# The order of the key tiles in a causal polynomial attention, and the engine of half of its masks

## The chip, the core and the metric

The kernel runs on one core of a Trainium2 chip. Time is device time in microseconds (us) for one launch, on the slowest core, which here is the only one. Lower is better. Before the change the median of three runs is 2473.38 us (2469.45 to 2477.04).

## What is computed

One block of a network on `x` of shape (4, 1024, 256), four sub-layers one after the other, each with a layer norm ahead of it and a residual sum behind it: a causal attention, a mixture of experts (16 experts, the best 6 for each token, and a shared one), a short convolution over the batch axis, and the same mixture once more. The attention has 16 heads of 16 numbers, rotary angles, a layer norm of each head's q and k, and a fourth power in place of the softmax:

```python
a = jnp.einsum('bhnd,bhmd->bhnm', q, k) ** degree      # degree = 4
a = jnp.tril(a)
denom = jnp.sum(a, axis=-1, keepdims=True)
return jnp.einsum('bhnm,bhmd->bhnd', a / denom, v)
```

So no maximum is subtracted and nothing runs along a row: the sums over keys may be taken in any order. The change touches the attention alone.

## The kernel before

**Tiling of the attention.** There are 8 pairs `u`: 4 batch rows by 2 groups of 8 heads. The 1024 queries are cut into an early half (`hf = 0`) and a late half (`hf = 1`) of 512. A *pass* is one pair and one half; the 8 early passes come first, then the 8 late ones. Within a pass the even and the odd heads (`a = 0, 1`) are done one after the other, four heads at a time; I call each of these a *list*. So there are 16 early lists and 16 late ones. A list runs over the key tiles `j` of 128 keys: four in the early half, eight in the late half. One key tile of one list is a *step*. Keys after a query do not count, so for the diagonal tiles (`j >= 4*hf`) only the queries from `n0 = (j - 4*hf)*128` on are computed: such a step is 512, 384, 256 or 128 queries wide, and its first 128 columns are masked. In the late half `j = 0..3` are 512 wide and unmasked. Before the change a list goes through `j` in rising order, so it ends on its narrow steps.

**One step.** `scores` (L686 and on) makes four matmuls, one for each head, on four strips of 32 rows of TensorE (L694), into two PSUM tiles `ps` of two heads each; there are only two such buffers, so the next step's scores must wait until ScalarE (ACT) has squared both of this step's tiles (L705). Then, for the diagonal steps, the first tile is masked on VectorE (DVE) by a product with the 0/1 tile `seen` (L712), and the second on GpSimd (POOL) by an `affine_select` (L714). The second squaring makes the fourth power: in the late half the first tile on DVE (L725), the second on ACT (L863); in the early half tile and parity of `j` decide among DVE, ACT and POOL (L727). `weigh` (L734 and on) multiplies by the values, four matmuls into one accumulator `acc` (L742), and after the last step of the list ACT copies `acc` out to `o_sb` (L751), which frees it for the next list. TensorE then turns `o_sb` into `po` (L764).

**The order of the work.** PE, DVE, ACT and the DMA queue of SP run in the order in which the program is written; so does POOL here in effect. Each turn of the main loop (L856 to L884) writes: the scores and first squares of step s+2 (`LOOK = 2`) with their masks and DVE squares; then some pieces of other work; then the ACT second square of step s+1 (L863); then `weigh` of step s; then more pieces of other work. An engine that waits for one operand holds up all that is written behind it on that engine.

**The other work** is cut into "bites" that are dealt out by the turn, not by time: the projections of q, k, v for a later pass (L571, two of four in each of two turns), their rotation and head norm on DVE (L593 to L623, with a root on ACT at L662), the transposes, the output projection (L794), and in the late half also the routing of the first half of the tokens for the mixture of experts (L273 to L391) and the scatter of their rows to the experts' queues in memory. These scatters are 96 indirect DMAs that POOL issues (L421), each about 1 us of POOL time. In the late half a chain for the next pass begins at the fourth step of a pass (`begin_chain`, L841).

The mixture stages after the attention (from about 765 us) are not touched.

Of the kernel before, what the change touches and what calls it, by code (L numbers as in the profile page):

```python
# [103 lines left out]
def block_kernel(  # L104
# [342 lines left out]
    with ExitStack() as actx:  # L447
# [238 lines left out]
        def scores(u, hf, a, j, last):  # L686

            n0 = max(0, (j - 4 * hf) * P)
            nq = 512 - n0
            kt = kT[u, j // 4]  # L690
            tiles = [PS["s"].tile([P, 2, 512], FP, tag="s", name="ps") for _ in range(2)]

            for h in (2, 0, 1, 3):
                nc.tensor.matmul(  # L694
                    tiles[h // 2][:, h % 2, 0:nq],
                    lhsT=kt[32 * h : 32 * h + 32, (j % 4) * P : (j % 4 + 1) * P],
                    rhs=qT[u, hf][a][32 * h : 32 * h + 32, n0:512],
                    start=True,
                    stop=True,
                )  # L700
            s2s, later = [], []
            masked = j >= 4 * hf
            for pr in range(2):
                s2 = sqp.tile([P, 2, 512], FP, name="s2")
                nc.scalar.activation(s2[:, :, 0:nq], tiles[pr][:, :, 0:nq], AF.Square)  # L705
                s2s.append(s2)
            for pr in range(2):
                s2 = s2s[pr]
                if masked:

                    if pr == 0:
                        nc.vector.tensor_mul(s2[:, :, 0:P], s2[:, :, 0:P], seen)  # L712
                    else:
                        nc.gpsimd.affine_select(  # L714
                            out=s2[:, :, 0:P],
                            in_=s2[:, :, 0:P],
                            compare_op=ALU.is_ge,
                            fill=0.0,
                            base=0,
                            pattern=[[0, 2], [1, P]],  # L720
                            channel_multiplier=-1,
                        )
                part = s2[:, :, 0:nq]
                if pr == 0 and (hf == 1 or j % 2 == 0):
                    nc.vector.tensor_mul(part, part, part)  # L725
                elif pr == 1 and hf == 0 and j % 2 == 1:
                    nc.gpsimd.tensor_mul(part, part, part)  # L727
                else:
                    later.append(part)
            return s2s, later  # L730
# [77 lines left out]
        passes = [(hf, u) for hf in range(2) for u in range(n_pairs)]  # L808

        def begin_chain(n):  # L810

            hf, u = passes[n]
            l, gp = pairs[u]
            if gp == 0:
                bites.need(NORM, (l, hf))
            bites.add(gp, qkv_bites(u, hf), n)
            if gp == 1 and n + 1 < len(passes):
                hf, u = passes[n + 1]
                l = pairs[u][0]
                bites.add(NORM, norm_bites(l, hf), (l, hf))  # L820


        later, powers = [], {}
        steps = [
            (n, a, j, 4 * hf + 3)
            for n, (hf, u) in enumerate(passes)
            for a in range(2)
            for j in range(4 * hf + 4)
        ]

        def forward(i):

            n, a, j, last = steps[i]
            hf, u = passes[n]
            if a == 0 and j == 0:
                bites.need(pairs[u][1], n)
            if hf == 0 and a == 1 and j == 0:
                begin_chain(n + 2)
            if hf == 1 and u > 0 and a == 0 and j == 3 and n + 1 < len(passes):

                begin_chain(n + 1)  # L841
            return scores(u, hf, a, j, last)

        with tc.manual_schedule(engines=ORDERED):
            with tc.tile_pool(name="ps_s", bufs=2, space=PSUM) as s, tc.tile_pool(
# [10 lines left out]
                for s in range(-LOOK, len(steps)):  # L856
                    bites.begin()
                    new = []
                    if s + LOOK < len(steps):
                        powers[s + LOOK], new = forward(s + LOOK)  # L860
                    bites.step(1, (1, 1, 1, 1, 1))
                    for part in later:
                        nc.scalar.activation(part, part, AF.Square)  # L863
                    later[:] = new
                    if s < 0:
                        bites.step(1, (2, 2, 1, 2, 1))
                        continue
                    n, a, j, last = steps[s]
                    hf, u = passes[n]
                    o_sb = weigh(u, hf, a, j, last, powers.pop(s))  # L870
                    bites.step(1, (2, 2, 1, 2, 1 if 0 not in plans or s % 2 else 0))
                    if o_sb is not None:
                        l, gp = pairs[u]
                        done = gather_bites(u, hf, a, o_sb)
                        if gp == 1 and a == 1:
                            done = chain(done, project_bites(l, hf))
                        bites.add(OUT, done)
                    if hf == 1 and not routed and not bites.lanes[OUT]:

                        routed = True  # L880
                        for i in range(TG):
                            bites.add(ROUTE, prepare(0, i, ap1, ps_m))
                        bites.add(ROUTE, chain(plan(0, ps_m), scatter(0, ap2, 1)))
# [437 lines left out]
```

## Time and profile before

| what | value |
|---|---|
| median of three runs | 2473.38 us |
| the profiled execution: its own time / its span | 2393.24 us / 2391.5 us |
| attention, first to last score (early half / late half) | 33.7 to about 285 us / 285 to 759 us |
| busy share of the span: PE, ACT, DVE, POOL | 88%, 52%, 47%, 38% |
| masks on DVE (L712), late half | 64, mean 427 ns |
| masks on POOL (L714), late half | 64, mean 687 ns |
| scatters issued by POOL (L421) in the attention | 96, mean 1048 ns |

The profiled execution took 80 us less than the median of the timed runs. The sums below are made against the profiled execution and then moved to the median.

A group line of the profile reads: line, engine, operation, output<-inputs, shape, count | busy us, mean ns of one | idle time of the engine just before, and which instruction's end released it. A timeline line reads: start, length, engine, line, operation, operands, count, and in brackets the idle time ahead and its releaser. The table of stretches gives for each stretch its length, then the busy time of each engine with its number of instructions in brackets, the clock granted to TensorE (1.00 is full), the DMA share and GB/s. A matmul's length in the timeline includes time in which its group waits for the second of its two PSUM tiles.

### The profile page before, as it was taken

To read this page: it belongs to the slowest core of one execution; us is meant where nothing else is said; L and a number is where in the kernel's file an instruction comes from. 1 tells how busy PE (TensorE), PEld (TensorE's weight loads), DVE (VectorE), ACT (ScalarE), POOL (GpSimd) and SP (SyncE) were. 2 spreads that over 40 slices of the span, in tenths; PEclk is the share of its full clock that TensorE was granted. 3 is DMA by queue.
4 is the path that set the end of the run, shared out by engine and by line. 5 is a ranking of instruction groups with operands and counts; after the bars stand their busy time and mean duration, and the time that the engine had idled before them with its cause. 6 is when DMAs were issued, how large, how long until landed. Compare 5 with 4: busy or idle time off the path is not lost.

```text
span 2391.5 us, 33033 instructions
## 1 busy us (share of the span) xinstructions
PE 2114.5 (88%) x10480; PEld 1308.4 (55%) x10480; DVE 1118.5 (47%) x2532; ACT 1240.2 (52%) x2754; POOL 901.4 (38%) x990
## 2 busy tenths in 40 slices
PE   5899999778898998999899999789999959999974
PEld 2344443222233466777666667567676747777632
DVE  5888867656555225111166652126754212441154
ACT  3677878566676145555455544335553424555410
POOL 3333211344431000444355226645513654540176
PEclk8888988889888999999999999989999979999987
DMA  7900000111101412555455335344423535663243
GB/s 232 342 7 1 1 1 1 38 51 45 53 27 62 114 48 79 165 166 166 137 151 154 102 104 176 132 139 142 145 92 121 176 124 154 202 186 115 91 123 112
DMA packets 212231, 267.73 MB, mean 112 GB/s; under 512 B 25280, under 2 KB 187232, under 8 KB 212064
## 3 DMA queue, kind: packets, MB, share of 16 engines
q1 hardware_dynamic: 166944, 161.04, 21.6%
q0 software_dynamic: 36992, 100.78, 13.4%
q10 hardware_dynamic: 8128, 3.80, 0.7%
q8 instruction: 91, 1.49, 0.3%
q14 instruction: 76, 0.62, 0.1%
HBM read 123.72 MB, written 141.82 MB: 111 GB/s over the span
## 4 chain that ended last, share of the span: by engine, by line
PE 67%; DVE 12%; issue 7%; ACT 7%; POOL 5%; DMA 2%; ACTq 0%; POOLq 0%; DVEq 0%; SPq 0%
PE pgu L1030 20%; PE py L1053 14%; PE ps L694 6%; PE acc L742 4%; PE pxt L1014 4%; PE pht L1044 4%; POOL xq L421 3%; PE pg L955 3%; ACT s L705 3%; PE pj L571 3%; PE pu L955 3%; PE po L972 3%; POOL yg L1147 2%; ACT s L863 1%; DVE X L1131 1%
## 5 line engine op out<-in xcount | busy, mean ns | idle before, releaser
L421 POOL DMA_INDIRECT xq<-sxn,sloti x384 | 379.2, 987 | 644.7 <-ACT xgT L1016 306.2
L1030 PE MATMUL pgu<-wgu,xgT 128*128 x1776 | 609.7, 466 | 4.4 <-DVE hbuf L1039 2.2
L1147 POOL DMA_INDIRECT yg<-yq,sloti x384 | 375.8, 979 | 421.8 <-issue 201.4
L1039 DVE TENSOR_TENSOR hbuf<-hbuf,pgu 128x176 f32<-128x176 f32 x444 | 149.4, 337 | 721.7 <-ACT hbuf L1038 721.2
L1030 PEld LDWEIGHTS pgu<-wgu,xgT 128*128 128x128 f32 x1776 | 338.7, 193 | 136.5 <-issue 20.3
L1038 ACT ACTIVATE hbuf<-pgu 128x176 f32<-128x176 f32 x444 | 141.4, 318 | 411.7 <-PE pgu L1030 411.6
L705 ACT ACTIVATE s<-ps 128x1024 f32<-128x1024 f32 (+3 forms) x384 | 291.4, 815 | 114.6 <-PE ps L694 113.5
L1053 PE MATMUL py<-w2a,hT 128*128 x888 | 268.7, 385 | 0.9 <-ACT yo L1062 0.9
L1053 PE MATMUL py<-w2b,hT 128*128 x888 | 266.4, 382 | 0.0
L1062 ACT COPY yo<-py 128x256 f32<-128x256 f32 x444 | 166.1, 374 | 167.0 <-PE py L1053 166.7
L1131 DVE SCALAR_TENSOR_TENSOR X<-yg,top,X 128x256 f32<-128x256 f32 x384 | 186.0, 484 | 87.8 <-DMA yg<-yq,sloti 81.8
L1014 PE MATMUL pxt<-ident,xg 128*128 128x128 f32 x888 | 171.8, 276 | 60.6 <-DMA xg<-xq 60.6
L714 POOL TENSOR_SCALAR_AFFINE_SELECT s<-s 128x256 f32<-128x256 f32 x128 | 84.2, 659 | 349.7 <-ACT s L705 349.5
L725 DVE TENSOR_TENSOR s<-s 128x1024 f32<-128x1024 f32 (+3 forms) x160 | 168.2, 1051 | 86.8 <-ACT s L705 83.5
L1016 ACT COPY xgT<-pxt 128x256 f32<-128x256 f32 x444 | 167.9, 378 | 68.7 <-PE pxt L1014 68.3
L694 PE MATMUL ps<-q,kA 32*128 32x512 f32 (+3 forms) x1024 | 182.0, 647 | 20.0 <-ACT s L705 18.0
L1044 PEld LDWEIGHTS pht<-ident,hbuf 128*128 128x128 f32 x888 | 125.9, 142 | 124.4 <-issue 71.1
L1053 PEld LDWEIGHTS py<-w2b,hT 128*128 128x128 f32 x888 | 170.2, 192 | 23.5
L863 ACT ACTIVATE s<-s 128x1024 f32<-128x1024 f32 x192 | 164.4, 856 | 27.5 <-POOL s L714 27.2
L1044 PE MATMUL pht<-ident,hbuf 128*128 128x128 f32 x888 | 171.6, 275 | 4.9 <-ACT hT L1046 4.9
L1046 ACT COPY hT<-pht 128x256 f32<-128x256 f32 x444 | 165.4, 372 | 1.7 <-PE pxt L1014 0.7
L742 PE MATMUL acc<-s,vA 128*32 128x512 f32 (+3 forms) x1024 | 140.1, 603 | 13.2 <-ACT s L863 10.8
(158 smaller groups left out, 2421.9 us busy)
## 6 DMA issues: line engine op xcount, KB each, us to landing
xg<-xq SPq DMA_DIRECT2D x148, 384.0 KB, 3.7
yq<-yo SPq DMA_DIRECT2D x148, 384.0 KB, 2.8
xq<-zero SPq DMA_DIRECT2D x74, 384.0 KB, 4.6
xq<-sxn,sloti POOLq DMA_INDIRECT x384, 2.4
yg<-yq,sloti POOLq DMA_INDIRECT x384, 2.9
wgu<-in_w SPq DMA_DIRECT2D x4, 1408.0 KB, 17.8
X<-in_x SPq DMA_DIRECT2D x8, 512.0 KB, 5.5
out<-X SPq DMA_DIRECT2D x8, 512.0 KB, 3.5
```

The lines of the kernel that those rows point to most:

```text
L421: d = nc.gpsimd.indirect_dma_start(out=xq[g][:, :], out_offset=bass.IndirectOffsetOnAxis(ap=sloti[:, c + i, k : k + 1], axis=0), in_=xs[:, ...
L694: nc.tensor.matmul(tiles[h // 2][:, h % 2, 0:nq], lhsT=kt[32 * h : 32 * h + 32, (j % 4) * P : (j % 4 + 1) * P], rhs=qT[u, hf][a][32 * h : ...
L705: nc.scalar.activation(s2[:, :, 0:nq], tiles[pr][:, :, 0:nq], AF.Square)
L725: nc.vector.tensor_mul(part, part, part)
L742: nc.tensor.matmul(acc[32 * r : 32 * r + 32, n0:512], lhsT=va[:, j % 4, h * VW : h * VW + 32], rhs=s2s[r // 2][:, r % 2, 0 : 512 - n0], st ...
L863: nc.scalar.activation(part, part, AF.Square)
L1014: nc.tensor.transpose(pt[:, k, :], xg[c][:, k * P : (k + 1) * P], ident)
L1030: nc.tensor.matmul(pg, lhsT=xT[c][:, k, :], rhs=wgu_f[k][:, bass.ds(vals[0] * (2 * FI), 2 * FI)], start=(k == 0), stop=(k == 1),)
L1044: nc.tensor.transpose(pt[:, k, :], hbuf[c % 4][:, k * P : (k + 1) * P], ident)
L1053: nc.tensor.matmul(py, lhsT=hT[c][:, k, :], rhs=w2_f[k][:, bass.ds(off[c] * E, E)], start=(k == 0), stop=(k == 1),)
L1131: nc.vector.scalar_tensor_tensor(X[:, t, l, :], yg[:, k, :], top[:, i, k0 + k : k0 + k + 1], X[:, t, l, :], op0=ALU.mult, op1=ALU.add,)
L1147: nc.gpsimd.indirect_dma_start(out=yg[:, k, :], out_offset=None, in_=yq[g][:, :], in_offset=bass.IndirectOffsetOnAxis(ap=sloti[:, i, k0 + ...
```

## The change

Two edits. First, each list takes its key tiles in a new order: 0, 3, 1, 2 in the early half (512, 128, 384, 256 wide) and 0, 7, 1, 6, 2, 5, 3, 4 in the late half (512, 128, 512, 256, 512, 384, 512, 512 wide, the masked ones at the second, fourth, sixth and eighth place). The last tile of the list, at which the accumulator closes, is taken from the table, and the late chains still begin at the fourth step of a pass. Second, in the late half the mask of the second PSUM tile goes to DVE as the product with `seen`, as that of the first tile does; the early half keeps its second masks on POOL.

```diff
-                    if pr == 0:
+                    if pr == 0 or hf == 1:
                         nc.vector.tensor_mul(s2[:, :, 0:P], s2[:, :, 0:P], seen)
                     else:
                         nc.gpsimd.affine_select(
...
+        turns = ((0, 3, 1, 2), (0, 7, 1, 6, 2, 5, 3, 4))
         steps = [
-            (n, a, j, 4 * hf + 3)
+            (n, a, j, turns[hf][-1])
             for n, (hf, u) in enumerate(passes)
             for a in range(2)
-            for j in range(4 * hf + 4)
+            for j in turns[hf]
         ]
...
-            if hf == 1 and u > 0 and a == 0 and j == 3 and n + 1 < len(passes):
+            if hf == 1 and u > 0 and a == 0 and j == turns[1][3] and n + 1 < len(passes):
```

In the built program PE, ACT and SP issue as many instructions as before; DVE issues 64 more (L712) and POOL 64 fewer (L714). In the late half POOL is then left with the copies of v (L582) and the scatters. Behind L824 the line numbers of the changed kernel are two higher (L863 becomes L865).

## The prediction

> **What bounds the kernel now.** I read the page first: PE is busy for 88% of the span, DVE 47%, POOL 38%. The change ends where the mixture stages begin, at about 765 us, so I took the busy time of each engine in four stretches of the attention: the early half, the late half without scatters, the late half with scatters, and its last lists.
>
> ```profile
> 34.00:285.00 251.00, 226.94 (x1464) 98.16 (x1460) 207.76 (x391) 180.63 (x309) 86.01 (x114) 0.89 0.36 121
> 285.00:450.00 165.00, 150.46 (x925) 58.66 (x928) 121.93 (x268) 128.37 (x179) 17.59 (x26) 0.89 0.00 1
> 450.00:690.00 240.00, 193.18 (x1127) 65.74 (x1124) 134.93 (x211) 160.95 (x221) 121.66 (x135) 0.86 0.15 53
> 690.00:765.00 75.00, 67.75 (x405) 20.93 (x403) 33.24 (x49) 58.10 (x77) 9.60 (x12) 0.82 0.01 2
> ```
>
> PE is busy 90, 91, 80 and 90% of these. The third row stands out: 47 us of PE idle, and POOL at 51%. Next, what ACT waits for in the late half (285 to 765 us):
>
> ```profile
> ACT s L705 <- PE ps L694: 78.6, 71, 3.3
> ACT s L863 <- POOL s L714: 27.2, 8, 8.3
> ACT h_vs L662 <- DVE h_vs L620: 11.8, 6, 3.9
> ```
>
> The second row is ACT's second square waiting for POOL's mask, 27.2 us in eight waits. The timeline at the longest one shows why POOL is late:
>
> ```profile
> 452.90 0.97 POOL L421 DMA_INDIRECT xq<-sxn,sloti  x1 [0.31 <-issue]
> ...
> 455.46 0.97 POOL L421 DMA_INDIRECT xq<-sxn,sloti  x1 [0.30 <-issue]
> 456.44 0.43 POOL L714 TENSOR_SCALAR_AFFINE_SELECT s<-s 128x256 f32<-128x256 f32 x1
> 456.89 0.84 ACT L863 ACTIVATE s<-s 128x768 f32<-128x768 f32 x1 [8.27 <-POOL s L714]
> ...
> 457.79 1.51 PE L742 MATMUL acc<-s,vB 128*32 128x384 f32 x8 [6.36 <-ACT s L863]
> 458.04 0.43 DVE L712 TENSOR_TENSOR s<-s,seen 128x256 f32<-128x256 f32 x1 [5.68 <-ACT s L705]
> ```
>
> The mask stands behind scatters in POOL's queue; ACT stands still for 8.27 us, PE for 6.36 us, and DVE, idle for 5.68 us, could have done the mask. Elsewhere there is a loop between PE and ACT (first row of the waits): both `ps` tiles must be squared before the next scores are complete. From a list near the end, with nearly no other work and at full clock:
>
> ```profile
> 727.36 1.94 ACT L705 ACTIVATE s<-ps 128x1024 f32<-128x1024 f32 x2 [0.28 <-PE ps L694]
> 730.31 1.51 ACT L705 ACTIVATE s<-ps 128x768 f32<-128x768 f32 x2
> 732.65 1.09 ACT L705 ACTIVATE s<-ps 128x512 f32<-128x512 f32 x2
> 734.37 0.66 ACT L705 ACTIVATE s<-ps 128x256 f32<-128x256 f32 x2
> 736.50 1.94 ACT L705 ACTIVATE s<-ps 128x1024 f32<-128x1024 f32 x2 [0.95 <-PE ps L694]
> ```
>
> Here one step is the time of its two squares and then the wait for the next scores: 727.36 + 1.94 = 729.30, and the next squares start 1.01 later; so 1.01 for scores 384 wide, 0.83 for 256, 0.63 for 128, and (from the squares at 712.33 to those at 715.50) 1.23 for 512.
>
> **Part 1: the new order, late half.** The sum of squares and scores is the same in any order: squares 5 x 1.94 + 1.51 + 1.09 + 0.66 = 12.96, scores 5 x 1.23 + 1.01 + 0.83 + 0.63 = 8.62, together 21.6 us a list. What differs is where ACT's second square (1.06, 0.86, 0.63, 0.42 us by width) or PE's `weigh` (1.06, 0.85, 0.64, 0.42) does not fit beside the squares. Before, at full clock: the step 128 wide takes 2.13 and not 1.89, since `weigh` of the 384 step does not fit (734.37 to 736.50), and the accumulator's copy (0.59) adds about 0.4: 22.2. After, step by step, in the new order from the 0th tile: 2.83 (the second square of the tile before, 1.06, is longer than scores of 128), 2.2 (`weigh` of 512 and then scores of 512 behind a square of only 0.66), 2.85 (transposes `po` 1.11, `weigh` 1.06 and scores), 2.35, 2.95, 2.75, 3.17, 3.17: 22.3. So the alternation is worth nothing at full clock: it pairs wide with wide, but the loop was never short of pairing. I take 0.
>
> The bites come by the turn, so their places hardly move: two turns with two projections (2.5 us of PE each turn) take 4.76 and 4.83 us now and I find 4.15 and 4.6 after, against bare steps of 3.17 + 3.17 and 2.35 + 2.95: the extra is 3.2 before and 3.5 after. The rotation and norm pieces (about 2.3 to 2.8 us of DVE in a turn) fall in steps of 384, 256 and 128 now, 6.2 us in all, and in steps of 384, 512 and 512 after, 9.1 us, with 3.0 us more of squares and masks to do; the root on ACT that waits for them (11.8 us in six waits) stays about as late. The DMAs of these stages are issued at the same turns. 0 again.
>
> **Early half.** PE is idle there for 24 us of 251, and ACT waits for PE more than PE for ACT. POOL's products fall on two neighbouring steps, where it needs 0.6 + 0.7 and 0.6 + 1.5 us against steps of 3.7 us on average, so they stay hidden. Bounds -5 to +5, I take 0.
>
> **Part 2: the masks.** POOL loses 64 x 687 ns = 44 us that lie off the path, except for the 27.2 us above. DVE gains 64 x 427 ns = 27 us in the late half, where it is busy for 290 of 480 us; of its 64 waits at a first mask 48 are for ACT, so it is usually early. But it is in order: the second mask stands behind the first mask and first square of its step (up to 2.1 us) and behind the bites of the turn before; behind ACT's second square stand the next squares, and behind those PE. In the new order a wide step (3.0 us or more) always follows a masked one before ACT asks for the mask, save between the last tile and the next list's first, both wide. Bounds: if DVE is never late, the gain is 27.2. In the order of before, a second mask on DVE would have ended 5.5 us late once (behind the routing's long pieces at 447 us), 2.3 us late twice and 0.7 once, and 3.1 of the 8.27 would have stayed: 14 us, which leaves 13. Nearer to the middle, since the wide step between gives slack: 20 us gained. What is late next is PE's own loop.
>
> A small extra: POOL's mask took 404 ns at its shortest and 687 on average while DVE worked. The Trainium skill ("GPSIMD Engine Reference", Key points) says that GpSimd shares its SBUF interfaces with VectorE and that DVE instructions with two SBUF inputs contend with it. DVE's squares are such instructions. By that rule both engines speed up when POOL has no masks. By the rows DVE's square of 512 does not (1.23 us with POOL idle, 1223 ns on average); that of 384 is 0.96 at best and 1180 ns on average over 16, so 3.5 us of DVE off the path. I book nothing.
>
> **Part 3: the clock.** The granted clock in the attention goes between 1.0 and 0.5:
>
> ```profile
> 710.00:716.80 6.80, 5.49 (x49) 1.86 (x50) 2.49 (x4) 4.72 (x8) 0.55 (x2) 1.00 0.01 2
> 716.80:723.60 6.80, 6.80 (x28) 2.02 (x27) 2.80 (x4) 4.94 (x6) 0.00 (x0) 0.50 0.00 0
> ```
>
> In the first row a wide square stands beside a narrow `weigh` twice, PE is idle for 1.3 us in pieces under 0.8 us, and half clock follows. A rule of the Trainium skill ("TensorE: Matmul & The Clock Gate", HAM oscillation) is to avoid PE idle gaps over some 3.4 us. By the rule only POOL's stalls cost clock, and removing four groups of them saves about 3 us (four half-clock stretches at some 0.9 us). By the row, each late list drops its clock once because its first two steps are thin on PE; a wide step then takes 4.11 (715.50 to 719.61) and not 3.17, and the list 24.2 (712.33 to 736.50) and not 22.2. The new order has thin steps too: in the first two (5.0 us) PE does about 3.8 us, and the half-clock stretch then meets `po`, a wide `weigh` and the scores in a row, which PE alone bounds: I put 2.6 us on it against 1.9 now. 0.7 x 16 = 11 us if every list has it; lists with bites in these steps escape, so 7. By the rule alone the total would be -23, by the row -16.
>
> **Sum.** -20 (masks) - 3 (stalls' clock) + 7 (thin steps) = -16 us: 2393 to 2377 in the profiled execution. The timed runs are 3.4% longer throughout; the same -16 there gives 2457.
>
> **Rivals.** *Nothing gained (0.22):* the waits for POOL turn into waits for DVE and for PE's loop; the lower bound of the masks, 13, against the full 11 of the clock: about 2471. For it: DVE is at 74% in the second stretch. Against: 48 of 64 waits at the first masks. *Slower (0.28), one mechanism:* the clock. If the first four steps of the new lists (10 us, thin throughout) hold PE under what keeps the clock up, each of the 16 late lists has one more half-clock stretch of 6.8 us at about 2.0 us, 32 us, against the 20: about +12 or more, 2486. It decides from about 1.2 us a list on. For it: all four steps mix thin and thick work, and 0.86 is already low. Against: the last four, now wide, are thick. *The change not doing what it says:* the built order shows it on PE, DVE and POOL as written, so I leave no chance for it.
>
> **Chances.** Forecast 0.50; a measurement of this kernel tells about 0.3% (7 us) from no change, so: faster 0.50, same 0.22, slower 0.28. The range reaches from both good bounds (-27 and -8: 2438) to the slower rival (2488). The forecast's own is 2438 to 2466.
>
> **What would show it.** ACT's second square waits for POOL 0 us, and for DVE under 10 us; the late half is 16 us shorter, nearly all of it where the scatters are; the early half within 5 us; POOL busy 44 us less, DVE 27 more; the clock of the late half at 0.85 to 0.87. Wrong if: the clock falls to 0.83 or below, ACT's waits for DVE pass 20 us, or bare lists move off 24 us.

## The result and the profile after

The changed kernel takes 2463.24 us (median of nine runs) against 2476.82 us before: ratio 0.9946, 95% interval 0.9930 to 0.9963, 13 us faster. The forecast was 16.

The kernel before takes about 2477 us in some sets of runs and about 2393 us in others, as in its first profile, and what decides it is open; so every ratio is within one set of runs, and "before" in a comparison with after is a second profile of that kernel, with a span of 2473.6 us.

ScalarE (ACT) in the late half waited for POOL's masks like this before (280 to 765 us; columns: total us, times, longest us):

```profile
ACT s L863 <- POOL s L714: 19.3, 4, 8.3
```

And this is what it waits for in the changed kernel (285 to 765 us):

```profile
ACT s L705 <- PE ps L694: 63.2, 84, 3.6
ACT h_vs L662 <- DVE h_vs L620: 13.0, 7, 4.0
...
ACT s L865 <- DVE s L712: 6.6, 3, 5.2
```

The waits for POOL's masks are gone; in their place stand 6.6 us for DVE's, 5.2 of them in one wait behind the routing's long pieces.

The early and the late half as two stretches, first before (profiled again), then after:

```profile
35.00:272.00 237.00, 214.26 (x1400) 93.73 (x1396) 197.42 (x375) 171.89 (x297) 85.13 (x113) 0.90 0.38 127
272.00:768.00 496.00, 421.55 (x2500) 149.19 (x2492) 296.76 (x536) 354.29 (x485) 149.14 (x174) 0.86 0.07 26
```

```profile
35.00:283.00 248.00, 212.98 (x1402) 96.23 (x1399) 203.15 (x374) 172.85 (x298) 85.50 (x114) 0.92 0.36 121
283.00:762.00 479.00, 407.66 (x2493) 148.30 (x2493) 314.70 (x601) 356.34 (x485) 113.55 (x108) 0.88 0.08 27
```

The late half is 17 us shorter, the early half 11 us longer. The clock of the late half rose from 0.86 to 0.88. In the profiles of this case it is only ever full or half, so 0.86 over 496 us is 139 us at half clock, and 0.88 over 479 us is 115. With the clock given to two digits, such a figure is good to about 5 us. The two spans differ by 4.4 us only (2473.6 and 2469.2), less than the medians do: the profile after is that of the slowest of the nine runs (2470.95 us).

A bare list, that is one with hardly any other work dealt out in it, near the end of the changed kernel: the squares of its first tiles in the new order and the next list's first, and the list as a stretch:

```profile
714.64 1.94 ACT L705 ACTIVATE s<-ps 128x1024 f32<-128x1024 f32 x2 [0.28 <-PE ps L694]
717.41 0.66 ACT L705 ACTIVATE s<-ps 128x256 f32<-128x256 f32 x2
719.76 1.94 ACT L705 ACTIVATE s<-ps 128x1024 f32<-128x1024 f32 x2 [0.27 <-PE ps L694]
722.50 1.08 ACT L705 ACTIVATE s<-ps 128x512 f32<-128x512 f32 x2 [0.50 <-PE ps L694]
724.81 1.94 ACT L705 ACTIVATE s<-ps 128x1024 f32<-128x1024 f32 x2 [0.28 <-PE ps L694]
...
736.83 1.94 ACT L705 ACTIVATE s<-ps 128x1024 f32<-128x1024 f32 x2 [0.28 <-PE ps L694]
```

```profile
714.60:736.80 22.20, 19.95 (x136) 6.18 (x140) 11.84 (x18) 19.58 (x25) 0.00 (x0) 1.00 0.00 1
```

The steps are 2.77, 2.35, 2.74, 2.31 us and so on, 22.2 us for the list, where the list before the change took 24.2. The forecast steps were 2.83, 2.2, 2.85, 2.35, and 22.3 in all. But that was the sum for full clock; the forecast put a half-clock stretch on top, and that stretch did not come: the clock of the row is 1.00.

### The profile page after: what moved, and what is told of

Its sections match the earlier page's. It is cut to its first block, busy times and chain, and to the rows that moved or that the text cites. A ratio compares the mean times of both kernels' runs of the same rounds, so it can differ in the third digit from the quotient of the medians.

```text
span 2469.2 us, 32975 instructions
## 1 busy us (share of the span) xinstructions
PE 2117.2 (86%) x10480; PEld 1314.8 (53%) x10480; DVE 1139.3 (46%) x2596; ACT 1238.5 (50%) x2754; POOL 864.2 (35%) x926
## 4 chain that ended last, share of the span: by engine, by line
PE 67%; DVE 17%; ACT 7%; issue 5%; another core or an unknown queue 2%; DMA 1%; POOL 1%; ACTq 0%; POOLq 0%; DVEq 0%; SPq 0%
PE pgu L1032 19%; PE py L1055 14%; PE ps L694 6%; PE pxt L1016 4%; PE pht L1046 4%; PE pg L957 3%; PE pu L957 3%; PE acc L742 3%; PE po L974 3%; PE pj L571 3%; ACT s L705 2%; DVE s L725 2%; DVE X L1133 2%; POOL xq L421 1%
## 5 line engine op out<-in xcount | busy, mean ns | idle before, releaser
L421 POOL DMA_INDIRECT xq<-sxn,sloti x384 | 385.6, 1004 | 776.7 <-ACT xgT L1018 302.9
L1055 PE MATMUL py<-w2a,hT 128*128 x888 | 274.1, 391 | 15.9 <-ACT yo L1064 8.7
L725 DVE TENSOR_TENSOR s<-s 128x1024 f32<-128x1024 f32 (+3 forms) x160 | 162.6, 1016 | 88.4 <-ACT s L705 71.6
L694 PE MATMUL ps<-q,kA 32*128 32x512 f32 (+3 forms) x1024 | 175.2, 643 | 15.3 <-ACT s L705 10.9
L1055 PEld LDWEIGHTS py<-w2b,hT 128*128 128x128 f32 x888 | 171.9, 194 | 24.2
L865 ACT ACTIVATE s<-s 128x1024 f32<-128x1024 f32 x192 | 163.8, 853 | 7.5 <-DVE s L712 7.4
L1016 PEld LDWEIGHTS pxt<-ident,xg 128*128 128x128 f32 x888 | 112.0, 144 | 69.2 <-issue 64.7
L1055 PEld LDWEIGHTS py<-w2a,hT 128*128 128x128 f32 x888 | 136.8, 195 | 21.9 <-ACT yo L1064 11.6
```

The lines of the kernel that those rows point to most:

```text
L421: d = nc.gpsimd.indirect_dma_start(out=xq[g][:, :], out_offset=bass.IndirectOffsetOnAxis(ap=sloti[:, c + i, k : k + 1], axis=0), in_=xs[:, ...
L694: nc.tensor.matmul(tiles[h // 2][:, h % 2, 0:nq], lhsT=kt[32 * h : 32 * h + 32, (j % 4) * P : (j % 4 + 1) * P], rhs=qT[u, hf][a][32 * h : ...
L1016: nc.tensor.transpose(pt[:, k, :], xg[c][:, k * P : (k + 1) * P], ident)
L1055: nc.tensor.matmul(py, lhsT=hT[c][:, k, :], rhs=w2_f[k][:, bass.ds(off[c] * E, E)], start=(k == 0), stop=(k == 1),)
```

## The experiments

Two theories stood after the result. **M**: the masks' move carries the gain, as predicted. **C**: the order carries it through TensorE's clock. Each run below has its ratio to the kernel before in the same set of runs, with the 95% interval.

**Before once more**, no edit. 

> The kernel before once more, for its profile: the first profiled execution took 2393 us where its timed runs took 2470 to 2480, and the profile after took 2469, so the two traces cannot be subtracted as they stand. Both theories: time within 0.3% of 1.000. If the 80 us are a matter of the single execution, the new profile has a span near 2470 and the mixture stages, which the change doesn't touch, are some 70 us longer than in the first one (about 1700 us and not 1631). The attention then ends near 761 us if it is free of this effect, and later, up to 775 us, if the effect is in the attention as well.

2476.93 us, ratio 1.0001 (0.9980 to 1.0022). The part behind the attention takes 1706 us here and 1631 in the first profile; the attention ends at 767.7 and not at 760.5. So the first profile can't be subtracted from the one after, and the timed runs are not "3.4% longer throughout", as the prediction has it: most of the 80 us lie behind the attention.

**The order alone.**

```diff
-                    if pr == 0 or hf == 1:
+                    if pr == 0:
```

> The new order in both halves, the late half's second masks left on GpSimd. Theory M (the masks carry the gain, as predicted, and the order is worth 0 to -7): no faster than before, ratio 0.999 to 1.004. Theory C (the order carries it, since the bare late lists now take 22.2 us and not 24.2 with the clock held at full): about 0.995, and the masks add little. The waits of ScalarE for GpSimd's masks should still be there, over 15 us in the late half.

2498.07 us, ratio 1.0080 (1.0054 to 1.0106): slower, by 20 us. Both theories missed. ACT's waits in its late half:

```profile
ACT s L865 <- POOL s L714: 30.1, 5, 9.3
ACT s L865 <- issue: 13.9, 3, 6.7
```

I read this as follows. In rising order the masks stand in the last four steps of a list, and POOL is free to run ahead with scatters in the first four. In the new order a mask comes at every second step, so each batch of scatters has a mask behind it that ACT needs soon. That the scatters are the cause is tested below. But they are not all of the 20 us: by the profiles the late half is 11 us longer than before (507 and 496), and the early half, which has the new order too, 12 us (249 and 237).

**The masks alone**: the condition above in the kernel before, with rising order. 

> The late half's second masks on VectorE, key tiles in rising order. Theory M: about -20 us, ratio 0.992. Theory C: -5 us or nothing, 0.998 to 1.000, since in rising order the narrow masked steps follow each other and VectorE's second mask is late, which puts 5 to 14 us of waits for VectorE in place of those for GpSimd.

2473.35 us, ratio 0.9978 (0.9958 to 0.9998): 5 us. The late half, and its second-last list:

```profile
276.00:766.00 490.00, 424.70 (x2494) 149.67 (x2492) 314.23 (x599) 354.85 (x485) 111.82 (x109) 0.84 0.08 27
...
716.70:740.80 24.10, 22.06 (x136) 6.37 (x136) 11.84 (x18) 19.56 (x25) 0.00 (x0) 0.86 0.00 0
```

The waits for POOL are gone here too, for 9.6 us of waits for DVE, but the half clock rose to 0.32 x 490 = 157 us, and the bare list still takes 24.1. So M does not carry the gain: 5 us and not 20.

Most of the missing gain was lost in one place. From one copy of the accumulator (L751) to the next, the sixteen late lists take 483.3 us in this profile and 489.1 before. Without the seventh they take 440.7 against 457.9, which is 17 us less. The seventh itself takes 42.6 us against 31.1. In it PE, DVE and ACT stand nearly still together from 479 to 487 us, for most of which POOL goes on issuing scatters, and for what ACT waits the profile says only "remote":

```profile
481.42 0.48 ACT L578 COPY qkv<-pj 128x384 f32<-128x384 f32 x1 [4.91 <-remote]
...
487.08 1.94 ACT L705 ACTIVATE s<-ps 128x1024 f32<-128x1024 f32 x2 [5.18 <-remote]
488.14 0.43 DVE L712 TENSOR_TENSOR s<-s,seen 128x256 f32<-128x256 f32 x1 [14.41 <-ACT s L705]
488.16 2.57 PE L694 MATMUL ps<-q,kB 32*128 32x384 f32 x8 [9.04 <-ACT s L705]
```

The seventh list takes 31 to 33 us in the three profiles with scatters and POOL's masks. With scatters and DVE's masks it takes 41.5 to 43.1 us in five profiles, that of the change among them (41.9), 35.3 and 38.5 in the two other late orders below, and 30.0 and 31.2 in the filler's and the last one. So it does not come with the masks' move alone. Its cause is open, and what the move is worth without it was not measured.

**The late order and the masks, early half rising.**

```diff
-        turns = ((0, 3, 1, 2), (0, 7, 1, 6, 2, 5, 3, 4))
+        turns = ((0, 1, 2, 3), (0, 7, 1, 6, 2, 5, 3, 4))
```

> As the changed kernel, but the early half in rising order. The profiles put the early half at 247 us after and 239 us before (first squares to the late half's first). If that is the early order's doing, this version is 8 us faster than the changed kernel: ratio to before about 0.991, early half 239 us. If it is the execution's, it is at 0.9946 like the changed kernel.

2459.34 us, ratio 0.9924 (0.9896 to 0.9952). Its late half:

```profile
275.00:745.00 470.00, 400.12 (x2500) 147.49 (x2492) 314.19 (x600) 355.92 (x485) 115.57 (x110) 0.91 0.08 28
```

Against the masks alone, the late order is worth 0.9924 / 0.9978, 0.5% or 13 us in time. In the profiles it is 20 us (490 and 470), but this one is of the fastest of its six runs (2450.32 us). Half clock is 0.18 x 470 = 85 us, down from 157. And the early order seems to cost something: 0.9946 against 0.9924, though these intervals overlap.

**The early order alone**, with the masks: `turns = ((0, 3, 1, 2), (0, 1, 2, 3, 4, 5, 6, 7))`. 

> Early half in the new order 0, 3, 1, 2, late half in rising order with its second masks on VectorE. The rest is as in the version with the masks alone (0.998), so what is added is the early order. From the profiles (early half 247 to 248 us in both kernels that have it, 236 to 240 in the four that have not) it costs 8 to 11 us: ratio 1.001 to 1.003. If the early half is only shifted work that later stages wait for anyway, 0.998.

2480.85 us, ratio 1.0005 (0.9990 to 1.0020): 7 us slower than the masks alone. In two ways, then, the early order costs 5 to 7 us, each time with intervals that overlap. The profiles are plainer: the early half takes 237 to 241 us in the seven with rising early order and 248 to 250 in the five with the new one.

**Turn-taking or the wide end?** Two late orders with the early half rising: `(0, 4, 1, 5, 2, 6, 3, 7)` and `(0, 1, 7, 6, 5, 4, 2, 3)`. 

> Late half 0, 4, 1, 5, 2, 6, 3, 7 with the second masks on VectorE, early half in rising order: masked and unmasked tiles still take turns, but the list ends on its narrowest tile, and one wide scoring (tile 4) stands beside the last list's narrow weighing (tile 7). Theory T (turn-taking keeps TensorE evenly busy, so its clock is halved for 80 us of the late half and not 140 to 157): one thin place is left in each list, so half clock 80 to 115 us, ratio 0.992 to 0.995. Theory W (what helps is that a list ends on a wide tile): like the masks alone, 0.998, half clock near 150 us.

> Late half 0, 1, 7, 6, 5, 4, 2, 3 with the second masks on VectorE, early half in rising order: the narrow tiles stand together in the middle of the list, which ends on a wide one. Theory T: the scorings of tiles 5 and 4 stand beside the narrow weighings of 7 and 6, two thin places in each list as in rising order, and the masks of four steps follow each other on VectorE: half clock 130 to 157 us, ratio 0.997 to 1.000. Theory W: like the late half's new order, 0.992.

The first: 2452.70 us, 0.9895 (0.9866 to 0.9925). The second: 2471.44 us, 0.9981 (0.9967 to 0.9995). So turn-taking gains without a wide end, and this order with a wide end and no turn-taking gains nothing over rising order. But the clock does not tell it all: the two have nearly the same half clock, 0.24 x 471 = 113 us and 0.22 x 493 = 108 us.

```profile
275.00:746.00 471.00, 413.97 (x2503) 149.61 (x2496) 313.98 (x601) 356.59 (x485) 113.87 (x110) 0.88 0.08 28
```

```profile
275.00:768.00 493.00, 421.14 (x2500) 152.41 (x2492) 314.54 (x600) 355.72 (x485) 106.27 (x109) 0.89 0.07 26
```

In the second order the chain for the next pass begins on the 256-wide tile, in the middle of the narrow block. Lists that carry such a chain take up to 39 us there; four of the six are 2 to 4 us longer than in the first order. I read this as other work dealt out by the step falling on short steps. No run tests it alone, and it is about half of the difference: three of the lists between are 3 to 5 us longer too.

**Another early order**, 0, 2, 1, 3, with the late half as in the change. 

> Late half as in the changed kernel, early half 0, 2, 1, 3. In the early half VectorE squares the even tiles, in rising order at the first and third step, in the new order at the first and fourth, right ahead of the head norm that ScalarE's root waits for (13.7 us of such waits before, 22.1 after). If that is why the new early order costs time, both squares at the first two steps leave the norm more room: root waits under 13 us, early half 232 to 238 us, ratio 0.990 to 0.992, no slower than the version with the early half in rising order (0.9924). If the loss comes from GpSimd's products on neighbouring steps (here the third and fourth), the early half stays at 245 us or more, ratio 0.995.

2460.65 us, 0.9924 (0.9900 to 0.9947). No slower than rising, but the early half is 243 us and the root waits are 19.2 us, not under 13: the reason I gave is not confirmed.

**A direct test of the clock**: rising order, masks on DVE, and TensorE given something to do in the two thin places of each list.

```diff
                     o_sb = weigh(u, hf, a, j, last, powers.pop(s))
+                    if hf == 1 and j >= 6:
+                        fill = ps_m().tile([P, 3 * P], FP, tag="m", name="fill")
+                        nc.tensor.matmul(
+                            fill,
+                            lhsT=ident,
+                            rhs=wqkv_sb[:, 0, 0].rearrange("p x g c -> p (x g c)"),
+                            start=True,
+                            stop=True,
+                        )
```

> Rising order with the second masks on VectorE (0.9978 so far), plus one product of 128x128 by 128x384 (0.6 to 1.2 us of TensorE, into a PSUM tile that nothing reads) behind each weighing of tiles 6 and 7 in the late half, where TensorE has waited for the wide squares of the next list. 32 products, 20 to 38 us of TensorE. Clock theory (the order gained because these two thin places of each list halve the clock): the halved clock in the late half falls from 157 to about 100 us, the bare last lists go from 24.2 to about 22.5 us, and the whole is 5 to 15 us faster than without, 0.992 to 0.996. Rival (the order gained by giving the other work longer turns to lie in, and the clock is only a companion): bare lists may shorten, but the whole is the same or slower, 0.998 to 1.008.

2351.89 us against 2393.64, ratio 0.9843 (0.9824 to 0.9861): 42 us faster than before with useless work added, the masks' move included, and well beyond what theory C expected. Its late half and its second-last list:

```profile
273.00:724.00 451.00, 409.37 (x2567) 149.56 (x2560) 314.90 (x600) 353.51 (x485) 115.37 (x110) 0.94 0.08 29
678.20:700.10 21.90, 20.90 (x140) 6.49 (x144) 11.84 (x18) 19.48 (x25) 0.00 (x0) 1.00 0.00 1
```

The bare list is the one shown for the masks alone, with two products more and the same work otherwise: 21.9 us at full clock and not 24.1 at 0.86. Half clock in the late half is 0.12 x 451 = 54 us. In this list, then, the thin places cost what the lower clock takes. How the 42 us divide is not shown: the masks alone were not timed beside the filler. Of the late half's 35 us (486 in the first profile, 451 here) the masks can give at most about 27, the whole of ACT's waits for POOL there.

**The scatters left out**, with the order and POOL's masks, and with the changed kernel as a control. In both the experts' share of the first mixture stage, for the first half of the tokens, is missing from the output.

```diff
                 i, k = divmod(j, TOPK)
+                if not send:
+                    continue
                 d = nc.gpsimd.indirect_dma_start(
...
-                        bites.add(ROUTE, chain(plan(0, ps_m), scatter(0, ap2, 1)))
+                        bites.add(ROUTE, chain(plan(0, ps_m), scatter(0, ap2, 1, False)))
```

> The new order with the late half's second masks on GpSimd (1.008 so far), with the 96 scatters inside the attention left out: the experts' queues of the first mixture stage hold zeros, so the experts' share of that stage is missing from the output. If the new order is slow with GpSimd's masks because these stand behind scatters at every second step, the waits for GpSimd's masks fall from 30 us (44 with those of unnamed cause) to under 5, and the time comes within 5 us of the same kernel with the masks on VectorE and no scatters. If GpSimd's mask itself is too slow for the new order, a gap of over 10 us stays.

> The changed kernel with the 96 scatters inside the attention left out (the same share of the output is missing). Control for the run before: with masks on VectorE the scatters cost the attention little, so at most 10 us faster than the changed kernel, 0.990 to 0.995; the gap to the run before is what GpSimd's masks cost when nothing stands ahead of them.

2367.75 us, 0.9899 (0.9880 to 0.9919), and 2372.91 us, 0.9920 (0.9905 to 0.9936). With nothing ahead of it POOL's mask makes ACT wait 0.2 us in the late half, and POOL is even 5 us better than DVE. So it was the queue, not the mask: with scatters the same pair stands at 1.0080 and 0.9946, and the mask on POOL is no shorter without them (762 ns on average, with them 722).

**Alternating engines in the early half**: `turns = ((0, 3, 2, 1), (0, 4, 1, 5, 2, 6, 3, 7))`. 

> Late half 0, 4, 1, 5, 2, 6, 3, 7 (the fastest so far, 0.9895 with the early half rising), early half 0, 3, 2, 1. Even tiles are squared by VectorE and odd ones by GpSimd in the early half; rising order alternates them, the two orders that cost 3 to 10 us there did not. If the split between the two engines is what the early order upset, 0, 3, 2, 1 alternates again and the early half is at 237 to 241 us, ratio 0.988 to 0.991. If it is something else about leaving rising order (widths, the place of the widest product on GpSimd), the early half stays at 243 us or more, ratio 0.991 to 0.995.

2366.13 us, 0.9891 (0.9871 to 0.9911), the ratio as hoped but not for the reason: the early half takes 251 us, the longest of all. The split of squares between DVE and POOL is not what the early order upsets.

## Why the total was right and its terms were not

**The bound.** The loop of squares and scores, its latencies and the sum of 22.3 us for a bare list at full clock were right to 0.1 us, and so was the claim that at full clock the order of the tiles is worth nothing (22.2 before by the forecast's sum, 22.2 measured after, 21.9 with the filler in rising order).

**Part 2, the masks.** ACT's waits for POOL went to nothing and those for DVE stayed under 10 us (6.6), as said. The size fails: "20 us gained" was 5.5 us when done alone (0.9958 to 0.9998, so 0.5 to 10). The sum set DVE's late masks against ACT's wait and had no term for anything else that could take the freed time. By the profile of the masks alone, fifteen late lists give 17 us and one takes 11.5 back in a standstill whose cause is open; half clock rose from 139 to 157 us on the way. The two edits also do not add up: with POOL's masks the order costs 20 us, with DVE's the late order gains. The forecast priced them one by one and never asked what the new order does to POOL's queue, because the masks were to leave it. DVE's busy time in the late half rose by 18 us and not 27; about 6 of the missing 9 are records that overlap, since the lengths add up to 24 us more. I had booked nothing for the rule on shared interfaces. The narrowest squares (256 elements) bear it out: 520 ns on average before and 552 with the order alone, 425 with the masks alone and after, 1.5 us in all and off the path. Those of 768 elements do not: 957 ns in the new order with POOL's masks as with DVE's.

**Part 3, the clock.** This step has the wrong sign. The prediction saw the thin first two steps in rising order and what they cost a bare list (2 us), and then wrote that "the new order has thin steps too" and put 7 us of loss on it. A bare list of the new order holds full clock throughout, and given DVE's masks the late order gains 13 us. The second-last list takes 22.2 us in all six profiles with this late order, with POOL's masks as with DVE's, and 24.1 to 24.4 in the four with rising order and no filler. That the clock carries all of the 13 us is not shown: two late orders above have nearly the same half clock and lie 19 us apart. The rule of long idle gaps that the prediction quotes would have missed it too: by that rule the filler, which closes only gaps under 1 us in the bare lists, does nothing, and it gave back 2.2 us a list.

The thin places themselves compare like this. The first two steps of a bare list after the change, in the same columns:

```profile
714.60:719.80 5.20, 4.20 (x33) 1.31 (x34) 2.42 (x4) 4.89 (x8) 0.00 (x0) 1.00 0.00 0
719.80:724.80 5.00, 4.67 (x40) 1.87 (x43) 3.27 (x6) 4.23 (x6) 0.00 (x0) 1.00 0.00 0
```

PE is busy for 81% of the first row, exactly the 5.49 of 6.80 us after which the clock fell before the change. What differs is that the next 5 us are at 93%. Busy time counts the waiting inside a group of products, so it can't rank such places; I had nothing better and took the pessimistic reading. What makes one of the two places lower the clock and not the other stays open.

**Part 1, the early half.** "I take 0", with bounds of 5 us either way, was wrong by 5 to 7 us of time. ACT's waits there, before (profiled again) and after:

```profile
ACT h_vs L662 <- DVE h_vs L620: 13.7, 4, 4.9
ACT qkv L578 <- PE pj L571: 9.3, 10, 1.3
```

```profile
ACT h_vs L662 <- DVE h_vs L620: 22.1, 7, 6.0
ACT qkv L578 <- PE pj L571: 15.6, 16, 1.6
```

The root behind DVE's head norm and the copies behind the projections come later, 15 us in sum. Two guesses at the cause (the place of DVE's second square, the alternation of DVE and POOL) did not hold in two other orders, 243 and 251 us; what makes rising order the best of the four there stays open.

**The sum.** Forecast -20 - 3 + 7 = -16, with 0 for the early half. Measured, as one chain of ratios: masks -5.5, late order given the masks -13, early order +5.5, together -13. So the masks came out 14.5 us worse than forecast, the early half 5.5 us worse, and the rest, which was to be +4 by the clock, 17 us better. That these errors cancel is luck. One of the prediction's own signs of being wrong came true: the bare lists moved off 24 us. Of the others, the late clock (0.88) lies above the 0.85 to 0.87 named, POOL is 36 us less busy and not 44, and the early half is 11 us longer and not within 5. The rival that the clock would decide was the right subject, with the sign turned.

**Versions that beat both.** The late order 0, 4, 1, 5, 2, 6, 3, 7 with the early half rising (0.9895), and the filler in rising order with DVE's masks (0.9843). Both together were not run.

## What to carry to other kernels

Where a profile shows the clock of an engine falling behind thin stretches, cost a reordering by where it thins that engine's work, and test it by filling the thin place with useless work: here that told more of the clock than three reorderings. Two edits that share a queue are not priced one by one; ask of each what it does if the other is left out. A wait that a change removes is worth its length only if nothing else, the clock included, closes in behind it.

## What the runs showed of the hardware

32 products that nothing reads, each in two halves (590 ns the median half; in the bare lists 0.91 us for both), made the kernel 42 us faster together with the masks' move. The granted clock of the late half was 0.94, before 0.86 to 0.87.

Half clock can follow a stretch without any long idle gap of TensorE. In the row from 710.00 to 716.80 us that the prediction shows, the longest gap is 0.76 us, and half clock follows. Of the 24 stretches of half clock in the late half of the first profile, 13 have no idle gap as long as 1 us in the 6.8 us ahead of them.

A mask of 128x256 on POOL behind scatters (about 1.05 us each) made ACT wait for up to 9.3 us. With the scatters left out the waits for it came to 0.2 us.
